# Diagonals of B written by small DMAs, SP's transfers in written order, and an earlier preparation in a selective scan

## The chip, the cores and the metric

The kernel runs on one core of a Trainium2 chip. The metric is device time in microseconds (us). A core has a matrix engine (TensorE, PE; its weight loads are shown as PEld), a vector engine (VectorE, DVE), a scalar engine (ScalarE, ACT), a general engine (GpSimd, POOL) and a queue engine (SyncE, SP), which here only issues DMAs. Each engine runs its own instructions in order, and the engines wait for each other through semaphores. Sixteen DMA engines move data between on-chip memory (SBUF) and DRAM; matmul results go to PSUM.

## The reference

Two layers run one after the other on x of 8 x 128 x 128 x 128. The change is in the second, a selective scan over the 16384 positions of each image (t below), with 256 inner channels d and 16 states n:

```
u = normalised output of layer 0            # 16384 positions x 128 channels
xs, z = split(u @ W_in)                     # 256 channels each
xc = silu(causal depthwise conv of 4 taps over xs + conv_b)
dt, B, C = split(xc @ W_xproj)              # 8, 16 and 16 columns
delta = softplus(dt @ W_dt + b_dt)
h[t, d, n] = exp(delta[t, d] * A[d, n]) * h[t-1, d, n] + delta[t, d] * xc[t, d] * B[t, n]
y[t, d] = sum over n of h[t, d, n] * C[t, n]
out = ((y + xc * D) * silu(z)) @ W_out      # then the residual is added
```

Layer 0 (Fourier and convolutional attention) is not touched.

## The kernel before, in words

**Tiling.** After layer 0 and the group norm, the scan part goes over 8 x 32 = 256 chunks of T = 512 positions. The 256 x 16 recurrences of a chunk are cut into 16 steps of two scans (`ST = 16`, `where`, line 1224). Step s belongs to half h = s // 8 of the channels, to the pair of states mp = s // 4 % 2 and to a block k = s % 4 of 32 channels. The 128 partitions of a step hold 4 groups of states (q) times 32 channels, and the two scans of a step take the two states of the pair (j).

**One step** (loop at line 1366). In this order the program writes: `keep_state(n-1)`, ACT copies the last column of the scan to `state`; `product(n+1)`, PE makes the input of the next scan, hb; the pieces in `first`; `decay(n+3)`, ACT makes two tiles dA = exp(delta * A); `scan(n)`, DVE runs the two recurrences from dA and hb into hs; the pieces in `beside` whose step is s; and `weigh(n)`, POOL multiplies hs by C into hc. hb has two buffers in PSUM, hs four, hc seven, dA ten.

**The product and the diagonals.** hb[(q, channel), t] = du[channel, t] * B[t, state]. PE forms it as a matmul over t: the weights are 64 rows of duT (du = delta * xc, turned so that t lies on the partitions), the moving matrix is `bd`, diagonal blocks of 64 x 64 with the values of B on the diagonal, the two states of a pair side by side. One product is 32 matmuls, each recorded twice. For every chunk and pair a new tile bd of 128 x 2048 numbers (8 KB a partition) is needed. `turn_b` (PE) turns B so that t lies on the partitions, `keep_b` (DVE) copies it to bt, `diagonals` (DVE) multiplies an identity (`same`) by B, one call for each mp and quarter j, and `more_diagonals` (ACT) does the same for single columns. Six of the eight quarters of a chunk are made on DVE, the other two on ACT in 16 instructions.

**Preparation.** While chunk i is scanned, chunk i+1 is prepared: `conv` (PE, taps into a bank) and `conv_act` (silu), `gate` (z), `xproj`, `xproj_act` (stores C to DRAM as cd and reads it back spread over the partitions as crep, `repeat_c`), `step_sizes` and `step_sizes_act` (delta, stored to DRAM as dld and read back spread as dlrep), `drive` (POOL, du), `turn` and `turn_act` (duT), and the diagonals. `norm` and the first conv taps already belong to chunk i+2. For the finished part of chunk i, `add` (PE) sums hc over states into y, `skip` (DVE) adds xc * D, `gated` (POOL) multiplies by the gate, `project` (PE) and `residual` (DVE) end it; some of these belong to chunk i-1. The list `beside` (line 1319) gives for every piece the step and the chunk relative to i.

**Order.** `InOrder` (line 169; its call is line 180, which nearly all instructions carry in the profile) ties the instructions of PE, DVE, ACT and POOL in the scan part to the written order. The DMAs that SP issues are not tied: a scheduler places them in the order in which their buffers come free. An eighth of the chunks also loads 2 MB of the residual's image (`rows_of`, acc, pieces of 128 bytes) and stores as much of the output (out, the same pieces, issued on ACT's queue). PSUM has four banks left beside hb (`bank`): bank 0 and 1 take turns between e_xc, e_z, e_x, e_dt, e_t and e_o, bank 2 holds e_bt for as long as the diagonals are made from it, bank 3 holds y.

Of the kernel before, what the change touches and what calls it, by code (L numbers as in the profile page):

```python
# [27 lines left out]
T = 512  # L28
# [83 lines left out]
def _layout(a):  # L112
# [46 lines left out]
    o["same64"] = np.tile(np.eye(64, dtype=np.float32), (2, 1))  # L159
# [31 lines left out]
def tile_kernel(ctx: ExitStack, tc: tile.TileContext, I: dict, out: bass.AP):  # L191
# [833 lines left out]
    with tc.tile_pool(name="e_c", bufs=1) as cp, tc.tile_pool(name="e_w", bufs=2) as wk, tc.tile_pool(  # L1025
# [10 lines left out]
        same = fixed("same", [128, ND], I["same64"])  # L1036
        unit = fixed("unit", [128, 128], I["consts"][:, 0:128])
        win = fixed("win", [128, 2 * DI], I["win"])
# [9 lines left out]
        wf = cp.tile([128, 4, DI], F32, name="wf")  # L1048
        nc.sync.dma_start(wf.rearrange("p a d -> p (a d)"), I["cw"].partition_broadcast(128))
        for k in range(4):  # L1050
            nc.vector.tensor_tensor(wf[:, k, :], wf[:, k, :], win[:, 0:DI], ALU.mult)
        state = cp.tile([128, NM, NBK], F32, name="state")
        ch = {}
# [4 lines left out]
        pe, dve, act, gps = (InOrder(tc, e) for e in (nc.tensor, nc.vector, nc.scalar, nc.gpsimd))  # L1058

        def load(i):  # L1060
            b, k = divmod(i, NCH)
            xin = wk.tile([128, T], F32, name="xin")
            nc.sync.dma_start(xin, X1[b, :, k * T : (k + 1) * T])
            ch[i] = {"xin": xin}

        def rows_of(b, r0):

            t = wk.tile([128, W, QR], F32, name="acc")
            nc.sync.dma_start(t, X1[b].rearrange("c (w h) -> c w h", h=H)[:, :, r0 : r0 + QR])
            image[b, r0] = t  # L1070
# [40 lines left out]
        def gate(i):  # L1111
            c = ch[i]
            c["sz"] = wk.tile([128, 2, T], F32, name="sz", bufs=3)
            for h in range(2):
                ps = bank("e_z", h)
                pe.matmul(ps, lhsT=win[:, DI + h * 128 : DI + (h + 1) * 128], rhs=c["u"][:, 3:], start=True, stop=True)
                act.activation(c["sz"][:, h, :], ps, AF.Silu)

        def xproj(i):
            c = ch[i]  # L1120
            ps = c["xp"] = bank("e_x", 0)
            for h in range(2):
                pe.matmul(ps, lhsT=wx[:, h, :], rhs=c["xc"][:, h, :], start=(h == 0), stop=(h == 1))

        def xproj_act(i):
            c = ch[i]
            c["dbl"] = wk.tile([128, T], F32, name="dbl", bufs=1)
            act.copy(paired(c["dbl"]), halves(c.pop("xp")))
            d = c["cd"] = dp.tile([DS, T], F32, name="cd")
            for x in range(2):  # L1130
                nc.sync.dma_start(halves(d)[:, x], paired(c["dbl"][64 + DS : 96, :])[:, x])
            repeat_c(i, 0)

        def repeat_c(i, mp):

            t = ch[i]["c", mp] = wk.tile([128, 2, T], F32, name="crep", bufs=3)
            for q in range(NQ):
                m = NM * q + 2 * mp
                to = t[q * NR : (q + 1) * NR].rearrange("p m t -> p (m t)")
                nc.sync.dma_start(to, ch[i]["cd"][m : m + 2].rearrange("m t -> (m t)").partition_broadcast(NR))  # L1140
# [8 lines left out]
        def step_sizes_act(i):  # L1149
            c = ch[i]  # L1150
            c["dl"] = wk.tile([128, 2, T], F32, name="dl", bufs=1)
            d = dp.tile([2, 128, T], F32, name="dld")
            for h in range(2):
                act.activation(c["dl"][:, h, :], c.pop(("dp", h)), AF.Softplus, bias=b_dt[:, h : h + 1])
            nc.sync.dma_start(d.rearrange("h p t -> p h t"), c["dl"])
            for h in range(2):
                if h:
                    repeat_c(i, 1)
                t = c["dlr", h] = wk.tile([128, 4, T], F32, name="dlrep")
                for q in range(NQ):  # L1160
                    nc.sync.dma_start(t[q * NR : (q + 1) * NR], d[h].rearrange("(k r) t -> r k t", r=NR))
# [7 lines left out]
        def turn(i, part):  # L1169

            c = ch[i]
            ps = c["tp"] = bank("e_t", 1)
            for j in range(2):
                for h in range(2):
                    to = ps[:, (2 * j + h) * 128 : (2 * j + h + 1) * 128]
                    t = (2 * part + j) * 128
                    pe.transpose(to, c["du"][:, h, t : t + 128], unit)
# [15 lines left out]
        def keep_b(i):  # L1193
            c = ch[i]
            c["bt"] = wk.tile([128, NTB, DS], F32, name="bt")
            dve.tensor_copy(c["bt"], c["bp"][:, : NTB * 32].rearrange("p (j n) -> p j n", n=32)[:, :, :DS])

        def diagonals(i, mp, j):


            c = ch[i]
            if (mp, j) in ((0, 0), (1, 0)):
                c["bd", mp] = wk.tile([128, NTB, NQ, ND, 2], F32, name="bd")
            to = [128, NQ, ND, 2]
            b = c["bp"][:, 32 * j : 32 * j + DS].rearrange("p (q m) -> p q m", m=NM)[:, :, 2 * mp : 2 * mp + 2]
            dve.tensor_tensor(
                c["bd", mp][:, j], same.unsqueeze(1).unsqueeze(3).to_broadcast(to), b.unsqueeze(2).to_broadcast(to), ALU.mult
            )

        def more_diagonals(i, which):  # L1210

            c = ch[i]
            for n in which:
                j, q, m = 2 + n // 8, n // 2 % 4, n % 2
                at = NM * q + 2 + m
                act.activation(c["bd", 1][:, j, q, :, m], same, AF.Identity, scale=c["bt"][:, j, at : at + 1])
# [14 lines left out]
        def decay(n):  # L1231
            i, h, mp, k = where(n)
            for j in range(2):
                dA = hp.tile([128, T], F32, name="dA", bufs=10)
                kk = 4 * h + k
                act.activation(dA, ch[i]["dlr", h][:, k, :], AF.Exp, scale=A[:, 2 * mp + j, kk : kk + 1])
                dAs[n, j] = dA
# [63 lines left out]
        def project(i):  # L1301
            c = ch[i]
            ps = c["o"] = bank("e_o", 1)
            for h in range(2):
                pe.matmul(ps, lhsT=wout[:, h, :], rhs=c["yt"][:, h, :], start=(h == 0), stop=(h == 1))

        def residual(i):
# [12 lines left out]
            (0, 1, lambda i: conv(i, 1, 2)),  # L1320
            (0, 0, lambda i: diagonals(i, 1, 1)),
            (0, 0, lambda i: more_diagonals(i, range(6, 11))),
            (1, 1, lambda i: conv(i, 1, 3)),
            (1, 0, lambda i: more_diagonals(i, range(11, 16))),
            (2, 1, conv_act),
            (2, -1, lambda i: add(i, 3, 0, 1)),
            (3, -1, lambda i: skip(i, 1)),
            (4, -1, lambda i: gated(i, 1)),
            (4, 1, xproj),
            (5, 1, xproj_act),  # L1330
            (5, 0, lambda i: add(i, 0, 0)),
            (6, 0, lambda i: add(i, 0, 1)),
            (6, 1, step_sizes),
            (6, 2, norm),
            (7, 1, turn_b),
            (8, -1, project),
            (8, 1, lambda i: drive(i, 0)),
            (8, 1, keep_b),
            (9, -1, residual),
            (9, 1, lambda i: drive(i, 1)),  # L1340
            (9, 2, lambda i: conv(i, 0, 0)),
            (10, 0, lambda i: add(i, 1, 0, 1)),
            (11, 0, lambda i: skip(i, 0)),
            (11, 1, lambda i: diagonals(i, 0, 0)),
            (11, 1, lambda i: turn(i, 0)),
            (11, 2, lambda i: conv(i, 0, 1)),
            (12, 0, lambda i: gated(i, 0)),
            (12, 1, lambda i: turn_act(i, 0)),
            (12, 1, lambda i: diagonals(i, 0, 1)),
            (12, 2, lambda i: conv(i, 0, 2)),  # L1350
            (13, 1, lambda i: diagonals(i, 0, 2)),
            (13, 1, lambda i: turn(i, 1)),
            (13, 2, lambda i: conv(i, 0, 3)),
            (14, 1, lambda i: turn_act(i, 1)),
            (14, 1, lambda i: diagonals(i, 0, 3)),
            (14, 0, lambda i: add(i, 2, 0, 1)),
            (15, 1, lambda i: diagonals(i, 1, 0)),
            (15, 1, lambda i: more_diagonals(i, range(6))),
            (15, 2, lambda i: conv(i, 1, 0, 1)),
        ]  # L1360
        first = [
            (3, 1, gate),
            (7, 1, step_sizes_act),
        ]
        LEAD = 3
        for n in range(-2 * ST, (total + 1) * ST):
            i, s = divmod(n, ST)
            if s == 0:
                if there(i + 2):
                    load(i + 2)  # L1370
                if there(i) and i % NCH * RT % QR == 0:
                    rows_of(i // NCH, i % NCH * RT)
# [35 lines left out]
```

## Time and profile before

| | |
|---|---|
| median of 3 runs | 18526.35 us (18518.2 to 18531.05) |
| the profiled execution | 18481.4 us, span on the core 18479.6 us |
| busy over the span | PE 89%, PEld 52%, DVE 77%, ACT 65%, POOL 71% |
| end of layer 0's last group norm | about 6564 us |
| first scan | 6617.5 us |
| DMA queues over the span | q1 (SP) 2206 MB, q10 (ACT) 277 MB, q8 (instructions) 45.6 MB |

How it is read: the table by stage gives the busy time of each engine in a stretch. A group line gives the engine, the operation, out<-in by the program's names and the shape, then the number of instructions, their busy time in us, the mean duration of one in ns, and the engine's idle time just before them with what ended it. Busy time counts overlapped instructions once, so it can be less than number times mean. A timeline line gives start, duration, engine, operation and tiles, the number of instructions merged into it, and in brackets the idle time before it. "issue" is time in which an engine waited for nothing that the profile shows. The granted clock (PEclk) is the share of full speed that TensorE got.

### The profile page before, as it was taken

To read this page: it belongs to the slowest core of one execution; us is meant where nothing else is said; L and a number is where in the kernel's file an instruction comes from. 1 tells how busy PE (TensorE), PEld (TensorE's weight loads), DVE (VectorE), ACT (ScalarE), POOL (GpSimd) and SP (SyncE) were. 2 spreads that over 40 slices of the span, in tenths; PEclk is the share of its full clock that TensorE was granted. 3 is DMA by queue.
4 is the path that set the end of the run, shared out by engine and by line. 5 is a ranking of instruction groups with operands and counts; after the bars stand their busy time and mean duration, and the time that the engine had idled before them with its cause. 6 is when DMAs were issued, how large, how long until landed. Compare 5 with 4: busy or idle time off the path is not lost.

```text
span 18479.6 us, 790974 instructions
## 1 busy us (share of the span) xinstructions
PE 16503.3 (89%) x353336; PEld 9529.9 (52%) x353336; DVE 14244.2 (77%) x15987; ACT 12009.6 (65%) x26077; POOL 13090.9 (71%) x7572
## 2 busy tenths in 40 slices
PE   7789988888888889999999999999999999999998
PEld 5566665566555544444444444444444444444444
DVE  5544544334444479999999999999999999999999
ACT  4443434334233358778778878888888878887887
POOL 3333334444222269999999999999999989998998
PEclk8889999988999999999999999999999999999999
DMA  9963337777776654444454445444544454445443
GB/s 375 371 235 89 96 106 248 240 230 218 207 204 192 186 139 100 103 96 100 97 105 101 100 96 108 99 99 98 106 98 99 100 103 100 99 98 105 98 98 88
DMA packets 2434566, 2601.34 MB, mean 141 GB/s; under 512 B 1221965, under 2 KB 1624013, under 8 KB 2396866
## 3 DMA queue, kind: packets, MB, share of 16 engines
q1 hardware_dynamic: 1730850, 2206.28, 43.9%
q10 hardware_dynamic: 679840, 277.32, 7.1%
q0 software_dynamic: 20480, 67.13, 1.1%
q8 instruction: 2783, 45.60, 1.1%
q14 instruction: 613, 5.02, 0.1%
HBM read 1715.23 MB, written 834.93 MB: 138 GB/s over the span
## 4 chain that ended last, share of the span: by engine, by line
PE 56%; DVE 22%; DMA 8%; issue 7%; ACT 6%; POOL 1%; SPq 1%; DVEq 0%; ACTq 0%; POOLq 0%
DVE hs L180 15%; PE hb L180 14%; PE y L180 8%; PE c_mm L180 6%; PE e_xc L180 4%; DVE bd L180 3%; PE e_z L180 3%; PE e_x L180 3%; PE d_b L180 2%; PE a_mm L180 2%; DMA d_of<-OFL 2%; PE c_gram L180 2%; PE d_p L180 2%; DMA X<-d_x 2%; ACT L180 2%
## 5 line engine op out<-in xcount | busy, mean ns | idle before, releaser
L180 POOL TENSOR_TENSOR hc<-hs,crep 128x1024 f32<-128x1024 f32 x4096 | 9653.4, 2377 | 982.4 <-DVE hs L180 858.1
L180 DVE TENSOR_TENSOR_SCAN hs<-dA,state,hb 128x512 f32<-128x512 f32 x7936 | 9611.4, 1269 | 558.2 <-PE hb L180 418.8
L180 PEld LDWEIGHTS hb<-bd,duT 64*32 64x32 f32 x262144 | 3727.5, 106 | 3971.3 <-issue 2808.4
L180 PE MATMUL hb<-bd,duT 64*32 64x128 f32 x262144 | 4919.3, 275 | 798.9 <-issue 417.8
L180 ACT ACTIVATE dA<-dlrep,A 128x512 f32<-128x512 f32 x8192 | 5443.8, 714 | 59.6 <-DMA dlrep<-dld 51.6
L180 PE MATMUL e_xc<-u,wf 128*128 128x512 f32 x4096 | 2263.9, 646 | 34.1 <-DVE A L1046 20.8
L180 PE MATMUL y<-hc,gath 128*32 128x512 f32 x16384 | 2053.4, 601 | 32.5 <-issue 31.2
L180 ACT COPY state<-hs 128x2 f32<-128x2 f32 x4096 | 775.9, 189 | 1676.2 <-DVE hs L180 1649.5
L180 ACT ACT_TABLE_LOAD x1057 | 1356.1, 1283 | 75.0 <-PE e_dt L180 40.1
L180 PE MATMUL c_mm<-src,taps 32*32 32x512 f32 x32768 | 1211.5, 626 | 191.8 <-issue 158.7
L180 DVE COPY vst<-c_mm 128x512 f32<-128x512 f32 x1024 | 685.0, 689 | 717.4 <-PE c_mm L180 620.6
L180 ACT ACTIVATE bd<-same,bt 128x64 f32<-128x64 f32 x4096 | 1054.0, 339 | 0.8 <-PE hb L180 0.8
L180 DVE TENSOR_TENSOR bd<-same,e_bt 128x512 f32<-128x512 f32 x1536 | 1036.7, 675 | 0.0
L180 PEld LDWEIGHTS c_mm<-src,taps 32*32 32x32 f32 x32768 | 681.2, 105 | 683.7 <-issue 493.5
L180 POOL TENSOR_SCALAR qm<-vst,cst 128x512 f32<-128x512 f32 x256 | 505.4, 2070 | 745.4 <-DVE vst L180 745.2
L180 ACT ACTIVATE junk<-vst 128x256 f32<-128x256 f32 x1024 | 416.4, 410 | 923.0 <-DVE vst L180 921.9
L180 PE MATMUL a_mm<-xt,wp 128*128 128x256 f32 x3072 | 760.6, 409 | 264.5 <-ACT pk L180 184.1
L180 POOL TENSOR_TENSOR eo<-eo,et 128x1008 f32<-128x1008 f32 x128 | 298.8, 2334 | 969.3 <-DVE et L180 960.8
L180 POOL DMA_DIRECT2D X<-d_x x256 | 139.1, 543 | 1069.5 <-DVE d_x L180 939.9
L180 PEld LDWEIGHTS e_xc<-u,wf 128*128 128x128 f32 x4096 | 654.7, 194 | 440.2 <-issue 436.1
L180 DVE TENSOR_TENSOR d_x<-d_p,d_x 128x512 f32<-128x512 f32 x256 | 274.9, 1074 | 780.3 <-DMA d_x<-in_x 490.0
L180 PEld LDWEIGHTS a_mm<-xt,wp 128*128 128x128 f32 x3072 | 619.3, 205 | 421.7 <-ACT pk L180 194.6
(179 smaller groups left out, 20011.2 us busy)
## 6 DMA issues: line engine op xcount, KB each, us to landing
dlrep<-dld SPq DMA_DIRECT2D x2048, 256.0 KB
crep<-cd SPq DMA_DIRECT2D x2048, 128.0 KB
dld<-dl SPq DMA_DIRECT2D x256, 512.0 KB
src<-Pq SPq DMA_DIRECT2D x128, 544.5 KB
src<-Pv SPq DMA_DIRECT2D x128, 544.5 KB
src<-Pk SPq DMA_DIRECT2D x128, 544.5 KB
src<-Px SPq DMA_DIRECT2D x128, 544.5 KB
xt<-in_x SPq DMA_DIRECT2D x64, 1024.0 KB
```

Of the source, the lines that this page charges most:

```text
L180: made = method(*args, **kwargs)
```

## The change

- bd is no longer computed. Four DRAM tensors (two chunks times two pairs, `diag`) are filled with zeros once. `keep_b`, now on ACT, copies B to bt, and four DMAs of 1024 pieces of 8 bytes write it onto the diagonals; `load_b` reads a whole bd (1 MB) back, twice a chunk. bd has three buffers.
- SP is tied to the written order as well.
- The preparation of chunk i+1 moves up by about two steps (and the conv by one to three), `gate`, `xproj` and all `add` are cut in halves in steps of their own, and the first half of every `add` stands two steps after the step of its last hc (before: three steps after, but for the first group, where it was two). `repeat_c(i, 1)` and the dlrep loads are pieces of their own. xin is loaded a chunk earlier, with one buffer; dA has nine buffers; some banks change.
- wf is made ahead of the loop from a temporary copy of half of W_in.

```diff
+    diag = {(n, mp): dram.tile([128, DROW], F32, name=f"diag{n}{mp}") for n in range(2) for mp in range(2)}
...
+        zero = zp.tile([128, DROW], F32, name="zero")
+        nc.gpsimd.memset(zero, 0.0)
+        for d in diag.values():
+            nc.sync.dma_start(d, zero)
...
-        pe, dve, act, gps = (InOrder(tc, e) for e in (nc.tensor, nc.vector, nc.scalar, nc.gpsimd))
+        pe, dve, act, gps, sp = (InOrder(tc, e) for e in (nc.tensor, nc.vector, nc.scalar, nc.gpsimd, nc.sync))
...
-            xin = wk.tile([128, T], F32, name="xin")
-            nc.sync.dma_start(xin, X1[b, :, k * T : (k + 1) * T])
+            xin = wk.tile([128, T], F32, name="xin", bufs=1)
+            sp.dma_start(xin, X1[b, :, k * T : (k + 1) * T])
...
-            nc.sync.dma_start(d.rearrange("h p t -> p h t"), c["dl"])
-            for h in range(2):
-                if h:
-                    repeat_c(i, 1)
-                t = c["dlr", h] = wk.tile([128, 4, T], F32, name="dlrep")
-                for q in range(NQ):
-                    nc.sync.dma_start(t[q * NR : (q + 1) * NR], d[h].rearrange("(k r) t -> r k t", r=NR))
+            sp.dma_start(d.rearrange("h p t -> p h t"), c["dl"])
+
+        def repeat_sizes(i, h):
+            c = ch[i]
+            t = c["dlr", h] = wk.tile([128, 4, T], F32, name="dlrep")
+            for q in range(NQ):
+                sp.dma_start(t[q * NR : (q + 1) * NR], c["dld"][h].rearrange("(k r) t -> r k t", r=NR))
...
         def keep_b(i):
             c = ch[i]
-            c["bt"] = wk.tile([128, NTB, DS], F32, name="bt")
-            dve.tensor_copy(c["bt"], c["bp"][:, : NTB * 32].rearrange("p (j n) -> p j n", n=32)[:, :, :DS])
+            bt = wk.tile([128, NTB, DS], F32, name="bt")
+            act.copy(bt, c.pop("bp")[:, : NTB * 32].rearrange("p (j n) -> p j n", n=32)[:, :, :DS])
+            for mp in range(2):
+                d = diag[i % 2, mp]
+                for x in range(2):
+                    ap = [[DROW + 2, ND], [2 * ND, NTB * NQ], [1, 2]]
+                    to = bass.AP(d.tensor, d.offset + x * ND * DROW, ap)
+                    frm = bt[ND * x : ND * x + ND].rearrange("p j (q m) -> p (j q) m", m=NM)[:, :, 2 * mp : 2 * mp + 2]
+                    sp.dma_start(to, frm)
+
+        def load_b(i, mp):
+            t = ch[i]["bd", mp] = wk.tile([128, NTB, NQ, ND, 2], F32, name="bd", bufs=3)
+            sp.dma_start(t.rearrange("p j q t m -> p (j q t m)"), diag[i % 2, mp])
-        def diagonals(i, mp, j):
-        def more_diagonals(i, which):
...
-                dA = hp.tile([128, T], F32, name="dA", bufs=10)
+                dA = hp.tile([128, T], F32, name="dA", bufs=9)
...
         beside = [
+            (0, 1, conv_act),
+            (0, 1, lambda i: gate(i, 0)),
+            (1, -1, lambda i: add(i, 3, 0)),
+            (2, -1, lambda i: add(i, 3, 1)),
+            (2, 1, lambda i: xproj(i, 0)),
+            (3, 1, lambda i: xproj(i, 1)),
+            (3, -1, lambda i: skip(i, 1)),
+            (3, 1, xproj_act),
+            (4, 1, turn_b),
+            (4, 1, step_sizes),
+            (4, 2, norm),
+            (4, 1, keep_b),
+            (4, -1, lambda i: gated(i, 1)),
+            (5, 0, lambda i: add(i, 0, 0)),
+            (5, 1, lambda i: repeat_sizes(i, 0)),
+            (6, 0, lambda i: add(i, 0, 1)),
+            (6, 1, lambda i: drive(i, 0)),
+            (6, 1, lambda i: load_b(i, 0)),
+            (7, 1, lambda i: drive(i, 1)),
+            (7, -1, project),
+            (8, -1, residual),
+            (8, 2, lambda i: conv(i, 0, 0)),
+            (9, 0, lambda i: add(i, 1, 0)),
+            (9, 2, lambda i: conv(i, 0, 1)),
+            (9, 1, lambda i: turn(i, 0)),
+            (10, 0, lambda i: add(i, 1, 1)),
+            (10, 1, lambda i: turn_act(i, 0)),
+            (10, 1, lambda i: load_b(i, 1)),
+            (11, 0, lambda i: skip(i, 0)),
+            (11, 1, lambda i: repeat_c(i, 1)),
+            (11, 2, lambda i: conv(i, 0, 2, 3)),
+            (12, 0, lambda i: gated(i, 0)),
+            (12, 1, lambda i: repeat_sizes(i, 1)),
+            (12, 3, load),
+            (12, 1, lambda i: turn(i, 1)),
+            (12, 2, lambda i: conv(i, 1, 0)),
+            (13, 0, lambda i: add(i, 2, 0)),
+            (13, 1, lambda i: turn_act(i, 1)),
+            (13, 2, lambda i: conv(i, 1, 1)),
+            (14, 0, lambda i: add(i, 2, 1)),
+            (14, 2, lambda i: conv(i, 1, 2)),
+            (15, 2, lambda i: conv(i, 1, 3)),
         ]
         first = [
-            (3, 1, gate),
-            (7, 1, step_sizes_act),
+            (1, 1, lambda i: gate(i, 1)),
+            (5, 1, step_sizes_act),
         ]
```

## The prediction

> **What bounds the kernel now.** First the table by stage, which shows where the change can act: the scan part runs from about 6564 us (end of the last group norm) to the end, 11916 of 18479.6 us. It makes 256 chunks of 512 positions, 16 steps each. One thousand microseconds of it:
>
> ```profile
> core 0: us, PE busy (x) PEld busy (x) DVE busy (x) ACT busy (x) POOL busy (x), PEclk, DMA share, GB/s
> 12000.00:13000.00 1000.00, 920.64 (x24458) 479.05 (x24461) 945.67 (x907) 802.37 (x1701) 916.61 (x434) 0.98 0.47 103
> ```
>
> DVE, PE and POOL are all above 91%, so relief of one uncovers another. Next the groups, shapes kept apart, between 8000 and 18400 us:
>
> ```profile
> L180 POOL TENSOR_TENSOR hc<-hs,crep 128x1024 f32<-128x1024 f32 x3598 | 8480.2, 2377 | 850.1 <-DVE hs L180 737.9 <-DMA dlrep<-dld 36.0 <-PE e_z L180 29.2
> L180 ACT ACTIVATE bd<-same,bt 128x64 f32<-128x64 f32 x3600 | 926.4, 339 | 0.8 <-PE hb L180 0.8
> L180 DVE TENSOR_TENSOR bd<-same,e_bt 128x512 f32<-128x512 f32 x1347 | 909.7, 675 | 0.0
> L180 POOL TENSOR_TENSOR du<-dl,xc 128x512 f32<-128x512 f32 x450 | 578.2, 1285 | 6.4 <-ACT dl L180 6.4
> L180 POOL TENSOR_TENSOR yt<-yt,sz 128x512 f32<-128x512 f32 x449 | 574.4, 1279 | 0.0
> ```
>
> hc comes 16 times a chunk, so 3598 are 224.9 chunks in 10400 us: 46.25 us each. In the timeline of SP's queue a chunk (one cd store to the next) takes 44.6 to 45.8 us, the seven from 10018.78 on 45.0 in the mean; eight that include one load of acc and one store of out take 370.7 (10384.74 to 10755.46). I call 45.0 the quiet chunk; the mean has 1.25 us more, 10 us per eight chunks. DVE bounds the quiet chunk: in its timeline a bd stands between two scan pairs six times, and each puts the next pair off by 0.58 us (pair ends 12024.43, next starts 12025.01).
>
> Third, the demand of the other two. PE, in order, where nothing holds it:
>
> ```profile
> 12034.69 1.16 PE L180 MATMUL hb<-bd,duT 64*32 64x128 f32 x64
> 12035.78 1.13 PE L180 MATMUL e_xc<-u,wf 128*128 128x512 f32 x2
> 12036.83 1.16 PE L180 MATMUL hb<-bd,duT 64*32 64x128 f32 x64
> 12037.92 1.92 PE L180 MATMUL y<-hc,gath 128*32 128x512 f32 x16
> 12039.77 1.16 PE L180 MATMUL hb<-bd,duT 64*32 64x128 f32 x64
> 12040.86 1.99 PE L180 MATMUL e_z<-u,win 128*128 128x512 f32 x4
> 12042.77 1.16 PE L180 MATMUL hb<-bd,duT 64*32 64x128 f32 x64
> ```
>
> Read starts, not durations: product plus one conv tap is 2.14 us, plus a whole add (16) 2.94, plus a whole gate 3.00. The same view gives 2.08 with a half add (8), 1.44 with turn_b, 2.53 with turn and a tap. Sixteen steps as written before: 41.1 us. Last, the final chunk, which has no preparation:
>
> ```profile
> 18422.94 14.16 DVE L180 TENSOR_TENSOR_SCAN hs<-dA,state,hb 128x512 f32<-128x512 f32 x12 [0.42 <-PE hb L180]
> 18425.61 14.06 POOL L180 TENSOR_TENSOR hc<-hs,crep 128x1024 f32<-128x1024 f32 x6 [0.27 <-POOL yt L180]
> ```
>
> A scan pair back to back is 2.36 us, a hc 2.343. POOL per chunk: 16 x 2.343 + 4 x 1.24 (du and yt, start to start) = 42.5.
>
> **The change, part by part.**
>
> *Diagonals.* DVE loses 6 x 0.58 + 0.2 (the bt copy) = 3.7 of 44 us: demand about 40.3 (16 x 2.36, plus two skips of 0.65 and a residual of 1.1). ACT loses 926.4/224.9 = 4.1 us and gains one copy of about 0.2; it was 80% busy, so that is worth nothing by itself. Without coupling the chunk falls from 45.0 to POOL's 42.5.
>
> *PE pieces.* By the same pitches the new steps are, 0 to 15: 2.14, 3.07, 3.07, 2.14, 2.50, 2.08, 2.08, 3.00, 2.14, 3.52, 2.08, 3.00, 2.53, 3.07, 3.07, 2.14: 41.6 us, 0.5 more, since split groups switch more often. Steps 0 to 2 before reached 2.94 with the 3.00 of step 3 after them; spreading matters only because PE may be late by one scan pair less a product, 1.3 us.
>
> *A wait that comes in.* add(1,0), add(2,0), add(3,0) move one step earlier, two steps after that of their last hc. At step 9, where hc 7 is needed, that costs. POOL has gated at step 4 and both drives now at steps 6 and 7, so hc 3 to hc 7 take 5 x 2.343 + 3 x 1.24 = 15.4 us. From the start of the product in step 2: 1.3 to its scan (12005.99 to 12007.30), 2.36 scan, 0.25 to hc 3, 15.4, 0.2 to add(1,0): 19.5 us. PE's own work on the same way, steps 2 to 8 and one product, is 18.1. PE waits 1.4 us; behind the add stand a tap, turn and the next product, and DVE waits for that. Chunk: 41.6 + 1.4 = 43.0. Nothing else closes a longer loop: adds at 13 and 17 follow no such cluster.
>
> *Transfers.* Per chunk two loads of bd, 1 MB each, and 4 x 1024 packets of 8 bytes come in. No row has 8-byte writes. The nearest are acc's 128-byte reads and out's 128-byte writes, each saturating the 16 engines:
>
> ```profile
> DMA packets 13581, 1.74 MB, mean 150 GB/s; under 512 B 13581, under 2 KB 13581, under 8 KB 13581
> ```
>
> (6563.4 to 6575 us): 13.7 ns a packet and engine. Out, 15918 packets in 15 us, gives 15.1 with other work beside it. Bounds per packet: 4 ns (it moves a sixteenth of the bytes) to 60 ns (four times the slower row, if tiny scattered writes cost more than their bytes); I take 14, the nearest row: 256 x 14 = 3.6 us of all engines, bounds 1 and 15. The loads add 5.6 (xt's 1 MB in the first slice run at 375 GB/s). The engines go from about 16 (share 0.47 of 46.25, less an eighth of acc and out) to 25 us of a quiet chunk. The results are due late: keep_b at step 4, product at step 15, 26 us away; so the transfers themselves are free. What they disturb is PE's instruction fetch, on queue q8 of the same engines (8.9 packets a chunk). Beside acc:
>
> ```profile
> 12221.14 0.64 PE L180 MATMUL hb<-bd,duT 64*32 64x128 f32 x24 [2.09 <-issue]
> 12229.19 0.92 PE L180 MATMUL hb<-bd,duT 64*32 64x128 f32 x45 [2.00 <-issue]
> ```
>
> Products broken off in the middle, waiting for nothing in the profile, 0.2 us per saturated microsecond. In the seven quiet chunks from 10000 to 10320 us such gaps are 9.8 us, 1.4 each. PE had 45.0 - 41.1 to absorb them. Scaled by the engines' time they become 2.2; a little over half falls into steps 2 to 8 (writes of the diagonals, dlrep, bd) and uses up the 1.4 us wait; 0.9 is added. Bounds for the part added: 0 and 4. **Quiet chunk: 43.9 us.**
>
> [...]
>
> *Order on SP.* In written order crep(1) at step 11 waits for hc 11 on POOL; behind it stand dlrep(1), xin, every eighth time acc, then the next cd. Their first users, norm and the exponentials on ACT, come 8 and 9 steps later: nothing while the delay is less. Acc (18 us) and out (19 us) now both meet the loads of bd. The 10 us per eight chunks were cushioned by PE's spare 3.9; I take 13, bounds 8 and 25: 1.6 a chunk.
>
> *Free edits.* Nine dA buffers: ACT's copy of state, ahead of the exponentials in its queue, already waits for the same scan (1432.6 us of waits). One xin: filled eight steps after its last reader. Prologue: 4 MB of zeros at 375 GB/s, 11 us, in place of a first acc that held the constants 11.7 us, plus a write and load of diagonals: +10, bounds -5 and +25.
>
> **Sum.** 43.9 + 1.6 = 45.5 against 46.25: 0.75 x 256 = 192 off, 10 on: 182 less than the execution's 18479.6 us span (18481.4 whole). The runs' median, 18526.35, is 45 us above that execution; off the median: 18345 us.
>
> **Rivals.**
> *Fetch does not suffer.* Chunk 43.0 plus 1.2 for acc and out: 44.2, 2.05 x 256 less 10: 18010. For: fetches are few and short. Against: gaps near every burst.
> *Coupling eats the gain.* PE and POOL at 97% with two product buffers leave another 0.7 us of waits: within 0.2%, 18490 to 18563. For: waits of DVE for hb already total 390.0 us in the window.
> *Slower: tiny writes choke the engines.* At 60 ns they take 15 us a chunk; at 0.2 us of gap per saturated microsecond PE loses 3.0 there, and 1.9 beside the rest (1.4 x 21.6/16), less the 1.4 wait: 43.0 + 3.5 = 46.5, acc and out 2.0 as their queues grow, 48.5: 18526 + 2.25 x 256 + 10 = 19110. It decides where 43.0 + 0.5 + 0.2 x 0.256 p + 1.6 passes 46.25, at p = 22 ns. Against: 128-byte packets show nothing like it.
> *The order backfires.* Late dlrep or bd in each eighth chunk, 25 us instead of 13 there, twice that if the next chunk is hit too: about 18650 to 18750.
>
> **Numbers.** Forecast 0.33, its own range 18200 to 18480; fetch rival 0.2; no change 0.14; tiny writes 0.19; order 0.14. Faster by over 0.2% (37 us, about what a measurement can tell): 0.53; same 0.14; slower 0.33. The range leaves out half of the fetch rival's case and most of the worst of the tiny writes: 18000 to 18900.
>
> **What would show it.** Right: no bd on DVE or ACT; DVE falls to about 89% with waits for hb in front of it; POOL about 94%; a PE wait for hc at the add of step 9; more "issue" gaps inside products. Wrong: long packets on the diagonal writes; waits of PE for bd or of ACT for dlrep; POOL's or PE's pitches changed; a lower granted clock than 0.98.

## The result, and the profile after

The change makes the kernel slower: 19276.83 us (median of four runs, 19261.13 to 19316.56) against 18528.7 us for the kernel before on the same chip, a ratio of 1.0408 (95% interval 1.039 to 1.0426). The forecast was 18345 us, in a range of 18000 to 18900. The profiled execution has a span of 19259.3 us, 779.7 more than before. Everything below counts between 8000 and 18400 us, as in the prediction.

The table by stage, same stretch as before (same columns):

```profile
12000.00:13000.00 1000.00, 905.81 (x23061) 445.69 (x23058) 826.61 (x713) 682.78 (x1307) 861.36 (x409) 0.98 0.66 138
```

DVE fell from 945.67 to 826.61 and ACT from 802.37 to 682.78, as meant. But POOL fell too, and PE is lower as well, though now nothing else is above it: no engine is the bound by its busy time. The DMA share rose from 0.47 to 0.66. The groups, shapes kept apart:

```profile
L179 POOL TENSOR_TENSOR hc<-hs,crep 128x1024 f32<-128x1024 f32 x3377 | 7943.8, 2376 | 1459.4 <-DVE hs L179 1314.8 <-DMA dlrep<-dld 74.3 <-DMA crep<-cd 28.8
L179 DVE TENSOR_TENSOR_SCAN hs<-dA,state,hb 128x512 f32<-128x512 f32 x6530 | 7858.4, 1262 | 1715.6 <-PE hb L179 1437.6 <-ACT dA L179 111.9 <-POOL hc L179 68.6
L179 ACT ACTIVATE dA<-dlrep,A 128x512 f32<-128x512 f32 x6754 | 4484.5, 713 | 343.9 <-DMA dlrep<-dld 338.4
L179 PE MATMUL hb<-bd,duT 64*32 64x128 f32 x216137 | 4240.7, 278 | 843.2 <-issue 697.1 <-DMA bd<-diag 125.3 <-DVE hs L179 2.1
```

3377 hc are 211.06 chunks in 10400 us, 49.28 us each, against 46.25: 3.03 x 256 = 776 us, nearly all of the 779.7. Follow the idle times back: POOL waits for the scan, the scan for PE's hb, and PE mostly for nothing that the profile shows. All waits of that kind (us in total, times, longest), the first two lines from the kernel before, the others from after:

```profile
DVE hs L180 <- PE hb L180: 390.0, 536, 4.5
PE hb L180 <- issue: 374.8, 259, 4.4
DVE hs L179 <- PE hb L179: 1527.8, 1085, 8.2
PE hb L179 <- issue: 697.1, 543, 4.0
```

The chain that ended last says the same: PE 73% (56% before), DVE 4% (22%).

Where in a chunk? SP's queue over one quiet chunk (start, duration, what is issued):

```profile
12004.03 0.77 SPq L179 DMA_DIRECT2D cd<-dbl  x2
12007.06 1.71 SPq L179 DMA_DIRECT2D crep<-cd  x4
12008.86 3.71 SPq L179 DMA_DIRECT2D diag<-bt  x4
12012.67 0.61 SPq L179 DMA_DIRECT2D dld<-dl  x1
12018.51 2.86 SPq L179 DMA_DIRECT2D dlrep<-dld  x4
12021.47 0.85 SPq L179 DMA_DIRECT2D bd<-diag  x2
12026.67 1.73 SPq L179 DMA_DIRECT2D crep<-cd  x4
12028.50 6.12 SPq L179 DMA_DIRECT2D dlrep<-dld  x4
```

Both loads of bd, written at steps 6 and 10, are issued together (12021.47, 0.85 us for the two): the later step in the program's text did not by itself delay the transfer. The same chunk in stretches of 4 us (the last three columns are granted clock, DMA share, GB/s):

```profile
12012.00:12016.00 4.00, 4.00 (x134) 2.10 (x132) 4.00 (x4) 4.00 (x10) 4.00 (x3) 1.00 0.88 73
12016.00:12020.00 4.00, 3.76 (x26) 1.30 (x31) 4.00 (x4) 2.30 (x6) 4.00 (x3) 1.00 0.41 93
12020.00:12024.00 4.00, 4.00 (x139) 2.29 (x133) 2.90 (x4) 2.22 (x6) 4.00 (x2) 1.00 1.05 232
12024.00:12028.00 4.00, 4.00 (x111) 2.29 (x115) 4.00 (x5) 2.43 (x5) 4.00 (x4) 1.00 1.00 360
12028.00:12032.00 4.00, 1.83 (x50) 0.64 (x39) 1.57 (x2) 2.06 (x5) 4.00 (x2) 0.87 1.03 302
12032.00:12036.00 4.00, 4.00 (x78) 1.55 (x74) 1.85 (x2) 1.43 (x3) 2.48 (x2) 0.71 1.03 212
12036.00:12040.00 4.00, 4.00 (x76) 1.48 (x68) 3.28 (x3) 1.46 (x4) 1.74 (x2) 1.00 0.58 130
12040.00:12044.00 4.00, 4.00 (x133) 2.37 (x132) 4.00 (x5) 3.09 (x5) 3.18 (x2) 1.00 0.02 5
```

For 18 us (12020 to 12038) all DMA engines are full (a share of about 1), then they are empty. In the middle of it PE is busy 1.83 of 4 us, and its clock falls to 0.87 and 0.71 in the stretches. PE's timeline there:

```profile
12030.72 0.55 PE L179 MATMUL hb<-bd,duT 64*32 64x128 f32 x12 [2.17 <-issue]
12031.19 1.93 PE L179 MATMUL y<-hc,gath 128*32 128x512 f32 x8
12033.05 1.75 PE L179 MATMUL e_xc<-u,wf 128*128 128x512 f32 x2
12034.73 1.16 PE L179 MATMUL hb<-bd,duT 64*32 64x128 f32 x64
```

A product breaks off for 2.17 us with no releaser, and the half add behind it takes 1.93 us, the conv tap 1.75 (start to start 1.86 and 1.68), while the next pair, at a granted clock of 1.00, takes 0.99 and 1.06 (starts 12035.82, 12036.81, 12037.87). So one gap is paid twice, as idle time and as the halved clock behind it. What PE waited for stands in the DMA records: queue q8 (kind "instruction") brings its instructions in blocks of 16 KB (1879 packets, 30.79 MB). One block ends at 12020.52, the next only at 12029.27, and the broken product goes on at 12030.72, 1.45 us after that.

From the trace's records I counted, for each run, two things per chunk: **gaps**, the distances over 0.25 us between starts of neighbouring matmuls inside one product; and **half clock**, the time at a granted clock of 0.5. "Rest" is the chunk less the gaps, less half of the half-clock time (that half of it is lost is an estimate: two matmuls of a conv tap start 1012 ns apart there in after, in the median, 854 in before, and 533 at full clock in both).

| run | ratio to before | chunk, us | gaps | half clock | rest |
|---|---|---|---|---|---|
| before | 1 | 46.25 | 2.0 | 1.3 | 43.6 |
| after | 1.0408 | 49.3 | 4.1 | 2.8 | 43.8 |
| e1_no_writes | 0.9992 | 46.1 | 2.4 | 0.9 | 43.3 |
| e2_no_loads | 0.9839 | 45.2 | 1.8 | 0.8 | 43.0 |
| e3_neither | 0.982 | 44.9 | 1.4 | 0.7 | 43.1 |
| e4_on_dve | 1.0392 | 49.2 | 1.4 | 3.1 | 46.3 |
| e10_writes_later | 1.0617 | 50.8 | 4.5 | 4.3 | 44.1 |
| e12_dma_only | 1.1081 | 54.2 | 3.7 | 8.8 | 46.2 |
| e14_dld_first | 1.0459 | 49.9 | 4.3 | 3.9 | 43.6 |
| e16_bd_apart | 1.0292 | 48.6 | 3.5 | 2.8 | 43.7 |
| e17_hold | 1.0136 | 47.3 | 3.1 | 1.8 | 43.3 |
| e22_dummy | 1.0529 | 50.2 | 5.3 | 3.6 | 43.1 |
| e27_all_three | 1.0372 | 49.2 | 4.6 | 3.0 | 43.0 |

e2 and e3 end before 18400 us and are counted to 18000. With two exceptions, told below (e4 and e12), the rest is 43.0 to 44.1 in every version, also in the seven that the table leaves out, whose gaps are 4.0 to 4.7. Beyond that the versions differ by gaps and half clock. That is the theory the experiments had to test: PE sets the end, and it loses time to the traffic itself.

### The profile page after: what moved, and what is told of

Its sections match the earlier page's. It is cut to its first block, busy times and chain, and to the rows that moved or that the text cites. A ratio compares the mean times of both kernels' runs of the same rounds, so it can differ in the third digit from the quotient of the medians.

```text
span 19259.3 us, 787363 instructions
## 1 busy us (share of the span) xinstructions
PE 17058.1 (89%) x353336; PEld 9491.4 (49%) x353336; DVE 13403.9 (70%) x14195; ACT 11063.1 (57%) x22237; POOL 13072.7 (68%) x7573
## 4 chain that ended last, share of the span: by engine, by line
PE 73%; DMA 10%; issue 8%; DVE 4%; POOL 3%; ACT 2%; SPq 0%; POOLq 0%; DVEq 0%; ACTq 0%
PE hb L179 22%; PE e_xc L179 10%; PE y L179 10%; PE c_mm L179 6%; PE e_z L179 3%; PE e_x L179 2%; PE a_mm L179 2%; PE d_b L179 2%; DMA d_of<-OFL 2%; DMA out<-acc 2%; PE c_gram L179 2%; POOL hc L179 2%; PE e_o L179 2%; PE d_p L179 2%; DVE hs L179 2%
## 5 line engine op out<-in xcount | busy, mean ns | idle before, releaser
L179 POOL TENSOR_TENSOR hc<-hs,crep 128x1024 f32<-128x1024 f32 x4096 | 9634.5, 2376 | 1792.2 <-DVE hs L179 1586.8
L179 PE MATMUL hb<-bd,duT 64*32 64x128 f32 x262144 | 5152.2, 278 | 1049.3 <-issue 851.9
L179 PEld LDWEIGHTS hb<-bd,duT 64*32 64x32 f32 x262144 | 3820.4, 107 | 4411.3 <-issue 3122.6
L179 PE MATMUL y<-hc,gath 128*32 128x512 f32 x16384 | 2403.7, 617 | 79.7 <-issue 51.2
L179 PE MATMUL e_xc<-u,wf 128*128 128x512 f32 x4096 | 2317.5, 659 | 43.8 <-issue 24.4
L179 ACT ACT_TABLE_LOAD x1057 | 1356.1, 1283 | 34.1 <-DMA dlrep<-dld 13.4
L179 ACT ACTIVATE sz<-e_z 128x512 f32<-128x512 f32 x512 | 306.1, 598 | 785.5 <-PE e_z L179 776.9
```

Of the source, the lines that this page charges most:

```text
L179: made = method(*args, **kwargs)
```

## The experiments

### Which half of the new traffic

e1_no_writes leaves out the writes of the diagonals after the first chunk (B stays at the first chunk's values), e2_no_loads loads bd once and uses it throughout, e3_neither does both.

```diff
 e1:
+                    if i < 1:
-                    sp.dma_start(to, frm)
+                        sp.dma_start(to, frm)
 e2:
-            t = ch[i]["bd", mp] = wk.tile([128, NTB, NQ, ND, 2], F32, name="bd", bufs=3)
-            sp.dma_start(t.rearrange("p j q t m -> p (j q t m)"), diag[i % 2, mp])
+            if i < 1:
+                kept[mp] = cp.tile([128, NTB, NQ, ND, 2], F32, name=f"bd{mp}")
+                sp.dma_start(kept[mp].rearrange("p j q t m -> p (j q t m)"), diag[i % 2, mp])
+            ch[i]["bd", mp] = kept[mp]
```

> The changed kernel without the 8-byte writes onto the diagonals (only the first chunk's are made, so B of the later chunks is wrong; every load stays). The steps of the changed kernel lose time at steps 12 to 15 and 0 to 1, not at 4 to 8 where the writes run. Theory (PE starves for instructions beside long bursts of loads): the writes cost only by holding dld, and so dlrep and bd, back by about 4 us; loads that come earlier meet PE's wait at step 9. Chunk 49.3 to about 48, 18850 to 19150 us. Rival (tiny writes choke the engines): chunk 45.5 to 46, 18350 to 18450 us.

> The changed kernel without the 1 MB loads of bd: one pair is loaded in the first chunk and used in all (so B is wrong), the 8-byte writes stay. Theory (bursts of loads): the losses at steps 12 to 15 fall from 4.3 us to under 2; chunk about 46.2, 18400 to 18600 us. Rival (tiny writes): no less than 18950 us. Rival (SP's written order delays the transfers): dlrep is as late as before, 18900 or more.

> The changed kernel with neither writes nor loads of diagonals (bd of the first chunk is used in all, B wrong): the order of the steps alone, with nothing of bd on DVE. Forecast's structure: PE 41.6 and the wait of 1.4 at step 9 make 43.0, and gaps as before the change (0.9 unabsorbed) and 1.5 for acc and out: chunk 45.0 to 45.5, 18180 to 18350 us. If the new order of steps or of SP were the cause of the slowdown, it stays above 18900 us.

Measured: 18451.67 us (0.9992, interval 0.998 to 1.0004), 18164.22 (0.9839, 0.9825 to 0.9854) and 18120.96 (0.982, 0.9802 to 0.9838), before at 18459.72. So the new order without the new traffic gains 1.8%, and the order is not to blame. The writes alone cost 43 us of it, the loads alone 331, both together about 1090 (1.0408 against 0.982), three times the sum of the two. All three forecasts missed, on the fast side. e1's number is that of the rival, choking writes (18350 to 18450), all but 2 us; e2, which keeps the writes and should then have taken 18950 or more, refutes that rival. PE's waits, of e1, e2 and e3 in this order (us in total, times, longest):

```profile
PE hb L179 <- issue: 415.9, 360, 3.2
```

```profile
PE hb L179 <- issue: 302.0, 291, 3.5
```

```profile
PE hb L179 <- issue: 254.2, 222, 3.8
```

After has 697.1 of these, in 543 waits. Without the writes the same transfers also lie differently. SP's queue of e1:

```profile
12009.07 0.38 SPq L179 DMA_DIRECT2D dld<-dl  x1
12012.68 2.90 SPq L179 DMA_DIRECT2D dlrep<-dld  x4
12015.67 5.90 SPq L179 DMA_DIRECT2D bd<-diag  x2
12026.82 1.73 SPq L179 DMA_DIRECT2D crep<-cd  x4
```

dlrep comes 3.6 us behind dld (5.8 in after, where dld lands among the writes), and the loads of bd are nearly through when the second crep comes: the DMA engines are full from 12014 to 12020 and from 12028 to 12036, and at 0.8 or less between.

### Order, waits and place of the writes

e4_on_dve keeps the new order of steps and SP's written order, and makes the diagonals on DVE and ACT at the old steps, from bt in SBUF. e9_sp_free takes SP out of the written order (`sp = nc.sync`). e11_no_dep sends the writes, from the third chunk on, to DRAM tiles that nobody reads. e5_add_late puts the sum of group 1 whole at step 10.

> The changed kernel with the diagonals made on DVE and ACT as before the change (from the copy in SBUF): order of the steps and of SP as changed, no DMA of diagonals. DVE's demand is back at 44 of a chunk, and PE's wait at step 9 stays. Theory (bursts of loads): chunk 46.0 to 46.8, about the time before the change, 18450 to 18700 us. Rival (order): 19000 us or more.

> The kernel after the change, with SyncE's transfers not tied to their written order any more (the other engines stay tied), so that the planner may put them where it likes. Theory (the burst, which the written order makes by holding dld, dlrep and bd behind the writes of the diagonals): 1.00 to 1.03 of the kernel before if the planner moves dld ahead of the writes, and no change (1.035 to 1.045) if it keeps the order. Rival (the order is innocent, the traffic costs): 1.035 to 1.045 with dld ahead of the writes too.

> The kernel after the change, with the writes of the diagonals from the third chunk on sent to four other DRAM tiles that nobody reads; the loads of bd read the tiles of the first two chunks again (so B is left at its first values). Bytes, packets and the order of issue stay, only the waits of loads for writes go. Theory (burst by order of issue): the loads waited for the order, not for the writes, so 1.03 to 1.045 of the kernel before. Rival (loads wait for the landing of the writes, or read slowly what has just been written in pieces of 8 bytes): 0.995 to 1.015, near the run without writes (0.9992).

> The kernel after the change, with the first half of the sum of group 1 at step 10 beside the second half instead of alone at step 9, so that TensorE does not wait there for hc of step 7 (step 9 takes 4.67 us in the mean, 3.67 at its fastest). Theory (TensorE sets the end and has nothing to spare): 0.7 to 1.4 us of each of 256 chunks come back, 1.022 to 1.033 of the kernel before. Rival (something else sets the end, the chain of transfers or GpSimd): 1.035 to 1.043, the wait only moves.

Measured: e4 19184.24 us (1.0392, 1.0376 to 1.0407), e9 19259.66 (1.0392, 1.0375 to 1.0409), e11 19239.1 (1.0374, 1.0354 to 1.0395), e5 19198.99 (1.0347, 1.0332 to 1.0363). The waits of loads for writes do nothing that stands clear of the noise (e11), nor does the written order of SP (e9; there crep is issued among the writes, and dld still comes behind them). The wait at step 9 is worth 0.6%, less than the theory's band and just short of the rival's: the rest falls by 0.7 us a chunk, as it should, but gaps and half clock take part of it back (4.3 and 3.3 us, 4.1 and 2.8 in after).

e4 needs a word, since its number is that of its rival and seems to blame the order that e3 cleared. It is a flawed experiment. Its group:

```profile
L180 DVE TENSOR_TENSOR bd<-same,bt 128x512 f32<-128x512 f32 x1271 | 1395.8, 1098 | 0.0
```

A diagonal made from bt in SBUF takes 1098 ns, one made from e_bt in PSUM took 675 in the kernel before: six of them cost DVE 2.5 us more a chunk. DVE is back at 94% (937.87 of 1000 us), and PE waits for it (us, times, longest), with 3.1 us of half clock:

```profile
PE hb L180 <- DVE hs L180: 533.3, 311, 3.4
```

Its rest, 46.3, is DVE's. POOL's hc is longer there too, 2465 ns against 2376 in after; why either is longer no run isolates.

Three runs move the writes on SP's queue: e14_dld_first to between dld and dlrep, e10_writes_later behind dlrep; e15_both is e14 with e5's edit.

```diff
 e14 (e10: the two lines in the other order)
+            (5, 1, write_b),
             (5, 1, lambda i: repeat_sizes(i, 0)),
```

> The kernel after the change, with the four writes of the diagonals moved on SyncE's queue from step 4, ahead of dld, to behind the four loads of dlrep of step 5; nothing else differs. Theory (the writes, 3.7 us of issue, hold dld and with it dlrep and bd back into the burst): dld and dlrep start 3 to 4 us earlier and run alone, 1.00 to 1.025 of the kernel before. Rival (the writes slow whatever runs with them or after them, wherever they stand): 1.035 or more, since their packets then run among those of dlrep and bd.

> The kernel after the change, with the four writes of the diagonals behind dld and ahead of dlrep on SyncE's queue, instead of ahead of dld (after) or behind dlrep (the run that came out at 1.0617). SyncE waits 5 us there for dld to land in any case, and issuing the writes takes 3.7 us. Theory (what counts is how late the chain cd, crep, writes, dld, dlrep, bd ends, since its tail falls together with crep, dlrep and bd of the second half): dlrep and bd start 3 to 4 us earlier, 1.00 to 1.03 of the kernel before. Rival (the packets of the writes slow what runs beside them, and now they run beside dld): 1.035 or more.

> The two edits before in one kernel: the writes between dld and dlrep, and the sum of group 1 whole at step 10. Theory: the gains add, 0.985 to 1.015 of the kernel before. Rival: 1.03 or more, as for each alone.

Measured: e10 19671.66 us (1.0617, 1.0597 to 1.0636), e14 19400.26 (1.0459, 1.0442 to 1.0477), e15 19510.5 (1.0519, 1.05 to 1.0539). All three are on the rivals' side. The theory of that moment, that the writes do harm by holding dld back, falls: with dld ahead of them it gets worse. The stretches of full engines moved with the loads (in e14 the losses are largest at steps 10 and 11, in after at 12 to 15) and even became shorter: the longest of a chunk lasts 13.3 us in e14 and 13.4 in e10 in the median, 17.1 in after. (Here and below the engines count as full while 14.4 of the 16 are busy, averaged over 1 us.)

e12_dma_only is the opposite of e4: the old order, only the diagonals by DMA (writes at step 8, loads at 11 and 15, two buffers).

> The kernel before, with only the diagonals changed: written by four small DMAs at step 8 and loaded at steps 11 and 15, none made on VectorE or ScalarE; the order of the steps, the preparation's lead and SyncE are those of the kernel before. Theory (the traffic of the diagonals does the harm, wherever the steps stand): 1.02 to 1.06 of the kernel before, with VectorE waiting for hb. Rival (the new order of the steps does it, as the run with the new order and the diagonals on VectorE, 1.0392, suggests): 0.98 to 1.01, the gain that VectorE's lighter load allows.

20553.63 us, 1.1081 (1.1065 to 1.1098), beyond the theory's band too. PE's waits there (us, times, longest):

```profile
PE hb L180 <- DMA bd<-diag: 940.6, 190, 17.8
PE hb L180 <- issue: 612.2, 299, 6.1
```

With two buffers and the writes at step 8, bd comes too late: 4.9 us a chunk of waits for it, 4.95 us each in the mean, and 8.8 us of half clock. The gaps rise as well, from 2.0 to 3.7 us. So most of this loss is waiting for data, and the run does not test the traffic alone. In after, with the preparation earlier and three buffers, PE waits 0.6 us a chunk for bd; which of the two does it no run separates.

### Breaking the stretch up, making it by hand

e8_spread cuts dlrep and bd into quarters and spreads them over steps 6 to 9 and 12 to 15. e16_bd_apart gives bd 1 one buffer and writes its load at step 14, so that it must wait for the last product of the chunk before. e20_even gives dlrep three buffers and loads both halves at step 5, and gives each bd one. e17_hold is e1, which has no writes, with a transfer of 1 KB ahead of dlrep 0 that must wait for du.

```diff
 e16:
-            t = ch[i]["bd", mp] = wk.tile([128, NTB, NQ, ND, 2], F32, name="bd", bufs=3)
+            t = ch[i]["bd", mp] = wk.tile([128, NTB, NQ, ND, 2], F32, name=f"bd{mp}", bufs=2 - mp)
-            (10, 1, lambda i: load_b(i, 1)),
+            (14, 1, lambda i: load_b(i, 1)),
```

> The kernel after the change, with the same bytes in another rhythm: the loads of dlrep and bd are cut in quarters of 64 and 256 KB and written at steps 6-9 (dlrep 0, then bd 0) and 12-15 (dlrep 1, then bd 1) instead of whole at 5, 6, 10 and 12, the load of xin at step 15. Theory (the burst: dlrep, both bd, crep and dlrep again fill all DMA engines in one stretch over steps 10 to 15, TensorE's instructions come late there, its clock is halved, and it has no time to spare): the burst is broken up, 0.985 to 1.01 of the kernel before (18180 to 18650 us), and TensorE's losses in steps 12 to 15 fall from 4.3 to under 2 us of a chunk. Rival (the bytes themselves, or the writes themselves): the same traffic costs the same, at or above 1.03.

> The kernel after the change with one load moved out of the long stretch: bd 0 keeps two buffers, bd 1 gets one, so that the load of bd 1, written at step 14 behind xin, must wait for the last product of the chunk before and falls into steps 15 to 2, where the DMA engines idle. Bytes, writes and all else stay. Theory (the unbroken stretch of 18 us in which all DMA engines are full delays TensorE's instructions, each gap then halves its clock): the stretch is 5 us shorter, 1.01 to 1.03 of the kernel before. Rival (the packets of 8 bytes do the harm, wherever the loads are): 1.035 to 1.045.

> The run without writes (0.9992, B frozen at the first chunk's) with its transfers held back by hand: a transfer of 1 KB that needs du of step 6 stands ahead of dlrep 0 and bd 0 on SyncE's queue, so that dlrep 0, bd 0, bd 1, crep and dlrep 1 come in one unbroken stretch as after the change, with no packet of 8 bytes anywhere. Theory (the unbroken stretch alone does it): 1.02 to 1.04 of the kernel before. Rival (the packets of 8 bytes are needed): 0.995 to 1.01.

> The kernel after the change with its loads laid evenly: dlrep gets a third buffer and both halves are loaded at step 5, bd has one buffer for each half, so that bd 0 waits for step 10 and bd 1, written at step 14, for the end of step 14. Bytes and writes stay. Theory (unbroken stretch): shorter stretches, 0.995 to 1.02 of the kernel before. Rival (packets of 8 bytes): 1.035 to 1.045. If bd 0 lands too late for the product at step 15, TensorE shows waits for bd and the time is above that of after whatever the theory.

Measured: e8 19124.41 us (1.0316, 1.03 to 1.0331), e16 19074.99 (1.0292, 1.027 to 1.0314), e17 18780.54 (1.0136, 1.0118 to 1.0154), e20 19546.66 (1.055, 1.0533 to 1.0568). e8's quarters were issued back to back (their steps delay nothing), but bd 1 now comes behind the second dlrep, and the stretch did become shorter: the longest of a chunk lasts 9.4 us in the median, 17.1 in after. It gave 0.9% back, not the 3% and more of the theory; the number is the rival's. e16 did what it should: in its queue bd 1 starts at 12019.76, behind the second dlrep (12012.74) and not with bd 0 (12006.51), the longest stretch lasts 9.1 us, and 1.1% comes back, inside the theory's band at its weak end. e20 misses both bands: all eight pieces of dlrep, bd 0 and crep are issued from 12036.43 to 12047.40, and the engines are full from 12040 on for 14 us or more; PE waits 191.9 us for bd there, 125.3 in after. e17 held less than meant (dlrep 3.2 us behind dld, 3.6 in e1) and settles nothing between theory and rival, whose bands it both misses. But it lost 1.4% against e1 without one 8-byte packet, with the same loads and a shift of less than 1 us: gaps of 3.1 in place of 2.4 and twice the half clock, at steps 10 and 11 as in e1.

### Traffic that nobody reads, and an earlier chain

e22_dummy is e2 with the loads put back into a tile that no engine reads. e26_earlier moves the chain from e_x to dlrep 0 one step up. e27_all_three joins e26, e16 and e5.

```diff
 e22, to e2:
+            else:
+                t = wk.tile([128, NTB, NQ, ND, 2], F32, name="dummy", bufs=1)
+                sp.dma_start(t.rearrange("p j q t m -> p (j q t m)"), diag[i % 2, mp])
             ch[i]["bd", mp] = kept[mp]
```

> The run without loads (0.9839: the products use the first chunk's diagonals throughout) with the loads put back, but into a tile that nobody reads. Every transfer of after is there, and no engine waits for bd. Theory (traffic alone: full DMA engines hold up TensorE's instructions, whoever reads the data): 1.03 to 1.045 of the kernel before, with TensorE's gaps without a releaser back at over 600 us of the window. Rival (the products wait for bd, or for a buffer of it): 0.985 to 1.01.

> The kernel after the change with the chain that feeds the transfers one step earlier: e_x at steps 1 and 2, its copy with cd and crep at 2, e_bt, e_dt and the four writes at 3, dld and dlrep 0 at 4. Writes 3 us later made 1.0459 and writes behind dlrep 1.0617. Theory (the earlier the chain, the more of it falls into the stretch in which the DMA engines idle, and the shorter the full one): 1.015 to 1.035. Rival (only the amount of traffic counts): 1.035 to 1.045.

> The three edits that helped or should help in one kernel: the chain one step earlier, bd 1 loaded after the end of step 14 (1.0292 alone), the sum of group 1 whole at step 10 (1.0347 alone). Theory: gains of 0.5 to 2.5, 1.1 and 0.6 per cent add to 0.995 to 1.02 of the kernel before; no version of this change is expected below 0.99. Rival (the gains are one and the same): 1.025 to 1.035.

Measured: e22 19523.12 us (1.0529, 1.0514 to 1.0545), e26 19187.89 (1.0349, 1.0329 to 1.037), e27 19228.15 (1.0372, 1.0355 to 1.0389). e22 is the run that decides between traffic and data. PE never waits for bd there, and its longest waits are:

```profile
PE hb L179 <- issue: 794.5, 565, 4.7
PE hb L179 <- ACT duT L179: 129.0, 26, 7.5
```

2 MB a chunk that nobody uses take the kernel from 0.9839 to 1.0529, more than the theory's band. (The tile has one buffer, so the second load waits for the first, which after does not do: in the chunk from 12030.12 us on the two take SP 8.62 us to issue, 0.85 in after. The place of the loads is therefore not quite that of after.) e26 gives 0.6% back, on the border of the two bands, and settles nothing; the gains of e5, e16 and e26 do not add (e27, outside both bands, is no better than e26). No version with all of the traffic beats the kernel before.

What the gaps wait for, the records of queue q8 settle. Between 8000 and 18000 us, 81% of the 586 gaps in after end 1.2 to 1.7 us after a block of instructions has landed; of the other matmuls in products only 10% start so. In the kernel before it is 94% of 294 gaps, in e1 98% of 403, in e22 81% of 636. And gaps come one block apart. Between 8000 and 18400 us after has 481024 of PE's instructions (matmuls and weight loads) and 1879 blocks, 256 a block; of the neighbouring gaps in after that lie less than 600 of PE's instructions apart, 89% lie 256 or 512 apart, within two. So the gaps are PE waiting for its next instructions, which come through the same 16 DMA engines (q8 has 1.3% of their time in after).

## Why the prediction was wrong

- **PE's demand, right.** Pitches of 41.6 us were forecast; the fastest tenth of each step, added up, is 41.8. The wait at step 9 was put at 1.4, the step at 3.52 + 1.4 = 4.92; its median is 4.97. "Quiet chunk 43.0" without gaps: the rest in the table is 43.1 for e3 and 43.8 for after. As forecast, DVE and ACT were relieved, and PE became the bound.
- **The transfers' size, right.** The 8-byte packet was taken at 14 ns: e2's share of queue q1 is 46.6% and e3's 39.8%, 6.8% of 10400 us over 223 chunks and 256 packets, 12.4 ns. Loads were to take 5.6 us of all engines; e1's 53.0% less e3's 39.8% is 6.1. The rival of choking writes (from 22 ns on) is wrong, although its 19110 is the nearest number of all: that is luck.
- **What is disturbed, right.** The prediction took the gaps for late instruction fetch; the blocks of q8 show it (81% of the gaps in after end 1.2 to 1.7 us behind one). The rival in which fetch does not suffer (18010) is wrong.
- **"The gaps become 2.2", wrong: the term that failed.** In quiet chunks (six of eight) gaps were 1.43 us before, as read; after they are 3.48. I scaled them with the engines' busy time. That time rose by half, as forecast (21.0 us a chunk before, 31.5 after, acc and out included), but the gaps rose 2.4 times. Where PE loses: behind the first 3 us of a full stretch 0.17 us per us, before and after alike (0.10 to 0.22 in all twenty versions), in those first 3 us 0.006 to 0.12; and there are 4.9 us a chunk of the former time before, 16.4 after. So the rate of 0.2 was near, but the time that it applies to more than tripled. This is no rule for placing transfers, though. In the thirteen versions with all of the traffic and the new order that time goes from 10.5 us (e27) to 17.5 (e9), and the gaps, 3.5 to 5.3, do not follow it: e27 and e9 have 4.6 and 4.7, and e22, with 12.5, has the most, half of them outside full stretches.
- **"Falls into steps 2 to 8 and uses up the wait", wrong.** Steps 3 to 6, beside the writes, lose 0.01 to 0.06 us each. The losses are in steps 12 to 1 (0.6 to 1.3 each), behind the wait, and the wait stays whole. SP's queue shows why: dlrep and bd start 14 us behind cd, at about step 8.
- **The halved clock, missing.** I named a lower clock as a sign, and gave it no price. Half-clock time is 1.29 us a chunk before and 2.78 after, 0.75 us of the loss if half of it is lost. (In the stretch of the first table the clock is 0.98 in both kernels; from 8000 to 18000 us it is 0.99 and 0.97.)
- **"The transfers themselves are free", nearly right as to data.** PE waited 125.3 us for bd and ACT 338.4 for dlrep in 211 chunks, 26 and 62 times; acc is loaded 26 times there. e22 shows that without any reader the loss is no smaller, though 26 waits of PE then come for duT.
- **Acc and out.** 10 us per eight chunks were to become 13: the other two of eight chunks take 48.79 before and 54.59 after, 6.8 and 14.1 us over two quiet ones (45.4 and 47.54). The prediction had 45.0 and 43.9 for the quiet chunk. Its rival of a backfiring order is added up wrongly: 12 us more in each of 32 chunks make about 18730, twice that about 19110, not 18650 to 18750.

Sum: the quiet chunk came out 3.6 us above its forecast; gaps are 2.6 of it (3.48 less the 0.9 counted), the clock 0.7 (half of 1.41 us), 0.4 is not assigned.

**Open.** The trace shows when a block of instructions moves, not when it is asked for; whether the request or the transfer is late stays open. Why writes and loads together cost three times the sum of their single costs is not shown. Nor is why the place of the transfers matters: e10 and e14 have shorter stretches than after and cost more; more of their gaps are over 3 us (86 and 88, 34 in after), and their half-clock time is longer (4.3 and 3.9 us a chunk, 2.8 in after). What makes gaps long no run shows.

## What to carry to other kernels

Price a transfer not only by its bytes and by who waits for its data. Here the DMA engines also bring the instructions of the engine that sets the end (8.9 blocks of 16 KB a chunk), and 2 MB a chunk that nobody read cost 7% beside the small writes. Two kinds of traffic that cost 0.2% and 1.8% alone cost 6% together, so test them together. Before work is moved from a busy engine to the DMA engines, look for the engine that will then be the bound, and count what gaps without a releaser it has already beside bursts, with the clock that follows each. A later step in the text did not hold a transfer back here (both loads of bd at 12021.47 in after); a wait for a buffer did (bd 1 in e16, issued 3.4 us after xin ahead of it), and one for data (dlrep, 5.8 us behind dld in after), so see in the queue's timeline when it really starts.

## What the runs showed of the hardware

- **After gaps over 2.2 us TensorE's clock was mostly halved.** Of the gaps inside products in after, none of 416 up to 1.7 us had a half clock begin within 5 us of its start; of 1.7 to 2.2 us, 22% of 74; of 2.2 to 3 us, 64% of 84; longer, 85% of 34. The other runs so counted (before, e1, e10) agree: 0 to 4%, 14 to 26%, 62 to 74%, 64 to 83%. A half clock lasts 3.4 or 6.8 us in 139 of the 140 records in after.
- **Traffic slowed compute that has no part in it.** The operation itself hardly changed (hb matmuls 278 ns after, 275 before); e22 shows that the supply of instructions suffered: 5.3 us of gaps a chunk against e2's 1.8, and 81% of its gaps end 1.2 to 1.7 us after a block of instructions has landed.
- **An 8-byte write cost about 12 ns** of one DMA engine (e2 against e3, above), no more than the 128-byte packets of acc and out (13.7 and 15.1 ns in the prediction's views).
